# Two relational graph-attention layers: layer 1's keys as columns of the dense products, its softmax by halves of a group, and stage 3's sums in one run

## Chip, core and metric

The kernel runs on one core of a Trainium2 chip. The engines named below are TensorE (PE; its weight loads are PEld), VectorE (DVE), ScalarE (ACT), GpSimd (POOL) and SyncE (SP); SP, ACT and POOL also issue DMAs. The metric is the device time of one execution in microseconds (us), lower is better.

## The reference

`x` is 3125 nodes by 768 features; 53,125 edges (25,000 in both directions and a loop at each node) are sorted by destination and have one of three types. Two layers follow each other, the first with four heads of 192 features and an ELU behind it, the second with one head of 768; then a residual and a layer norm.

```python
xr = einsum('nd,rdf->rnf', x, W)          # three dense products per node
oi, oj = xr[etype, dst], xr[etype, src]   # rows of both ends
alpha = leaky_relu(oi @ q + oj @ k, 0.2)  # a score per edge and head
m = segment_max(alpha, dst)
e = exp(alpha - m[dst])
a = e / (segment_sum(e, dst)[dst] + EPS)
out = segment_sum(a[:, :, None] * oj.reshape(-1, heads, out_ch), dst) + b
```

## The kernel before

Nodes go in 25 blocks of 128. Edges go in 25 groups: group `b` holds up to 17 slots of 128 edges (14 in group 0), and the nodes whose edges it holds. In a slot, the 128 edges lie on the 128 partitions. float32 is multiplied in two parts (`H` and `L`): each product of a block is three matmuls for each of the six 128-feature tiles, so 18 in all.

Four stages follow each other. All instructions are issued in an order written out by hand: each stage has a table `ev` that `when(k, f, ...)` fills, and a loop over `k` that runs what stands under `k` in the order of entry. Each engine takes its own instructions in this order, and waits where the next one's inputs or buffers are not ready.

*Weights and keys.* `weights_kq` loads the 18 tiles of `W1`, splits them into `wH` and `wL`, and multiplies them by `k` and `q`, so that `wk` holds, per relation and head, the vector that gives a node's key or query from `x`. `nodes_kq` then runs over all 25 blocks of `x`: it turns the block (PE transposes), multiplies it by `wk` (L301), puts the keys into the DRAM table `kt1`, and keeps the queries in `qq`. Between these, `first` computes block 0's dense products, 18 pieces of six matmuls, seven of them while `weights_kq` still runs.

*Stage 1* (`phase1`). `d_products` (L750) multiplies blocks 1 to 24 by the 2304 columns of `wH`/`wL`, in pieces of 512 and one of 256 columns over two PSUM banks; `d_row` copies a piece into a row buffer and writes finished rows to the DRAM table `tab1`. A row of `tab1` has, for each of four heads, 192 features and a 1.0, so that a weighted sum of rows also gives the sum of the weights. Beside it run, for groups 0 to 20: the gather of keys, one indirect DMA of 16 bytes an edge per slot (`a_gather`), issued by POOL; the queries (`a_q`, `a_q2`, `a_q3`); the scores, three transposes, two running maxima, exponential and transpose back (`a_alpha`, `a_max`, `a_scan`, `a_back`). The results are the weights `pall`. `w_load` and `w_split` prepare `W2` here.

*Stage 2* (`phase2`). At step `k` POOL gathers slot `k` from `tab1` (L489) into a ring of 14 row buffers. Five steps later `sums` (L1047) adds the slot's rows into the group's nodes: a matmul of 32 columns for each place (a slot and one of the four windows of 32 nodes that it may touch) and head, the four heads side by side in the PE. Its weights `selp` come from `high` (L481), four or eight DVE instructions a slot, three steps ahead. Behind a group's last slot: `e_y` (divides, adds the bias, L1060), `e_x` and `e_h` (ELU), `h_row` (L1126, four writes of the result into layer 2's table `tab2`), `e_t` (turn, L1077), `e_s` and `e_s2` (the two parts `hT`, L1084 to L1099), and layer 2's products for two relations and its keys and queries (L1154), whose 18 steps `d_part` stand between the slots of the next group; `d_row` copies them and writes the rows (L1188) and a tail (L1177), and `d_q` splits the queries into three parts (L156 to L161). All seven writes of a group go into `tab2` at a position read from a register. The last four groups' keys are gathered in stage 2 (`LATE`, `KEYS`, `KEY_AT`), and their softmax runs there (`l_load` to `l_put`), with buffers borrowed from `y`, `ey` and `pt`.

*Stage 3* (`phase3`). Gathers from `tab2` into a ring of 31 rows. The key is column 769 of a row, so scores come from gathered rows (`a_alpha`, L1372). `a_spread` (L1338) and `a_spread2` (L1344) make the selection for the queries in five parts; `a_q2` (L1358), `a_turn` (L1381), `a_scan` (L1387 to L1392), `a_exp` (L1396), `a_back` (L1400), `marks` (L1406), `weigh` (L1420). `sums` (L1433) adds rows in two halves `c` of 384 columns over two PSUM tiles `acc`; `r_own` (ACT, L1444) and `r_other` (DVE, L1450, z in L1455) part the result into R and A, `r_turn` (L1483), `r_high` (L1494) and `r_low` (L1499) turn A, and `d_products` (L1517) multiplies it by the third relation of `W2`. Then residual, layer norm, output. With `e` the step behind a group's last slot, the order is:

```python
for d, f in ((2, a_alpha), (3, a_turn), (4, a_scan), (5, a_exp), (6, a_back), (7, weigh)):
    when(e + d, f, b)
for c in range(2):
    for n in range(8):
        when(e + 9 + 3 * c + n // 3, sums, b, c, n)
    for d, f in ((13, r_own), (13, r_other), (14, r_turn), (15, r_high), (15, r_low)):
        when(e + d + 3 * c, f, b, c)
```

## Time and profile before

| | us |
|---|---|
| median of 2 runs | 2199.07 |
| lowest and highest | 2196.68, 2201.46 |
| the profiled execution | 2202.57 |
| its span, first to last instruction | 2200.7 |
| mean granted PE clock of the span | 0.932 |

The profile is of one execution. Times in it are counted from the first instruction. A line such as "L1060" is a line of the kernel before; a tile is named without its buffer number. In a group, "x100: 406/409/419" is the count and the shortest, middle and longest duration in ns, followed by the first and the last start. A piece of the timeline or of the chain of waits has its start, its length, and in brackets the idle time of the engine before it and what ended that. float32 matmuls of the sums pass through PE twice and have two records each.

### The profile page before, as it was taken

What the parts mean: (1) busy time and instruction counts of PE and PEld (TensorE: products, weight loads), DVE (VectorE), ACT (ScalarE), POOL (GpSimd) and SP (SyncE); (2) the same over time, 40 slices, a digit from 0 to 9 for tenths busy, and PEclk for the clock granted to TensorE, in tenths of its full rate; (3) what the DMA queues carried; (4) which work ended last, traced back from release to release, by engine and by line L of the source; (5) the groups of instructions that cost most, each with busy time, mean ns of one, the idle gap of its engine ahead of it and who ended that gap; (6) DMA issues with size and microseconds to landing.
All of it is one profiled execution on the core that took longest, in us unless ns stands there. A gap on an engine that the chain in (4) does not pass through costs nothing.

```text
span 2200.7 us, 42790 instructions
## 1 busy us (share of the span) xinstructions
PE 1919.3 (87%) x14921; PEld 1328.3 (60%) x14921; DVE 1356.9 (62%) x4864; ACT 443.5 (20%) x978; POOL 1347.3 (61%) x1326
## 2 busy tenths in 40 slices
PE   8999999999979998897979989918888888888886
PEld 7877888778756655554546555704555555555554
DVE  7557566566568765775657657425655656566663
ACT  6412222222101111111111101101222222222222
POOL 4277777777657777665656545054655656666660
PEclk9999999999989999898989989958999999999998
DMA  7476556555878888786868877396878878788880
GB/s 234 146 198 194 182 181 193 173 180 178 268 252 270 280 285 275 223 258 197 261 221 266 253 220 250 126 286 198 267 262 261 270 263 270 262 266 263 273 274 24
DMA packets 173959, 506.28 MB, mean 230 GB/s; under 512 B 52687, under 2 KB 73794, under 8 KB 173733
## 3 DMA queue, kind: packets, MB, share of 16 engines
q0 software_dynamic: 81936, 331.52, 48.4%
q1 hardware_dynamic: 83135, 160.64, 21.4%
q10 hardware_dynamic: 8662, 11.29, 1.6%
q8 instruction: 119, 1.95, 0.4%
q14 instruction: 107, 0.88, 0.1%
HBM read 412.45 MB, written 95.69 MB: 231 GB/s over the span
## 4 chain that ended last, share of the span: by engine, by line
PE 51%; DMA 28%; DVE 13%; ACT 4%; issue 2%; SPq 1%; POOL 1%; POOLq 0%; ACTq 0%; DVEq 0%
PE po L750 16%; DMA ftab<-y 15%; PE acc L1433 12%; PE D L1517 10%; DMA ftab<-r 4%; DVE selp L481 4%; PE po L1154 3%; PE acc L1047 2%; DMA y<-ed_d 2%; DMA kt<-kt,ridx 1%; PE bc L1338 1%; PE bank L301 1%; ACT R L1444 1%; DVE y L1060 1%; DMA d<-dr_d 1%
## 5 line engine op out<-in xcount | busy, mean ns | idle before, releaser
L489 POOL DMA_INDIRECT kt<-kt,ridx x374 | 401.7, 1074 | 121.7 <-issue 71.6
L489 POOL DMA_INDIRECT G<-ftab,ridx x314 | 317.9, 1012 | 201.2 <-PE acc L1433 131.3
L489 POOL DMA_INDIRECT share<-ftab,ridx x299 | 303.3, 1014 | 207.5 <-PE acc L1047 126.6
L750 PE MATMUL po<-wH,xT 128*128 128x512 f32 (+1 forms) x1320 | 391.2, 377 | 0.4 <-DVE xT L729 0.4
L481 DVE TENSOR_SCALAR selp<-frow,fdl,pall 128x32 f32<-128x32 f32 (+1 forms) x1688 | 378.1, 324 | 18.5 <-DMA share<-ftab,rfirst 6.6
L1154 PE MATMUL po<-wH,hT 128*128 128x386 f32 (+1 forms) x1200 | 368.4, 369 | 0.3 <-ACT r L1183 0.3
L1433 PE MATMUL acc<-G,marks 128*32 128x384 f32 (+1 forms) x2520 | 294.7, 493 | 25.5 <-ACT A L1444 25.5
L1154 PEld LDWEIGHTS po<-wH,hT 128*128 128x128 f32 x1200 | 216.7, 193 | 90.7 <-issue 77.9
L750 PEld LDWEIGHTS po<-wH,xT 128*128 128x128 f32 x1320 | 240.2, 190 | 45.9 <-DVE xT L729 1.3
L750 PE MATMUL po<-wL,xT 128*128 128x512 f32 (+1 forms) x660 | 247.0, 374 | 0.0
L1517 PE MATMUL D<-w,AT 128*128 128x512 f32 (+1 forms) x900 | 225.8, 399 | 21.5 <-DVE AT L1499 21.5
L1047 PE MATMUL acc<-share,selp 128*32 128x193 f32 x2936 | 199.5, 351 | 26.5 <-DVE selp L481 26.3
L1154 PE MATMUL po<-wL,hT 128*128 128x386 f32 (+1 forms) x600 | 219.0, 365 | 0.0
L1433 PEld LDWEIGHTS acc<-G,marks 128*32 128x32 f32 x2520 | 142.6, 110 | 126.4 <-ACT A L1444 40.8
L1517 PEld LDWEIGHTS D<-w,AT 128*128 128x128 f32 x900 | 158.3, 216 | 61.1 <-DVE AT L1499 29.0
L489 POOL DMA_INDIRECT g<-ftab,ridx x135 | 137.3, 1017 | 60.9 <-PE acc L1047 39.9
L1344 DVE TENSOR_SCALAR sT<-bc,cols 128x512 bf16<-128x512 f32 (+1 forms) x125 | 82.9, 663 | 121.5 <-PE bc L1338 121.5
L1183 ACT COPY r<-po 128x384 f32<-128x384 f32 (+3 forms) x125 | 49.4, 412 | 537.2 <-PE po L1154 342.0
L1047 PEld LDWEIGHTS acc<-share,selp 128*32 128x32 f32 x2936 | 81.9, 112 | 107.3 <-DVE selp L481 57.6
L1433 PE MATMUL acc<-share,marks 128*32 128x384 f32 (+1 forms) x464 | 136.9, 490 | 3.5 <-ACT A L1444 3.5
L750 PEld LDWEIGHTS po<-wL,xT 128*128 128x128 f32 x660 | 125.0, 189 | 22.3
L1154 PEld LDWEIGHTS po<-wL,hT 128*128 128x128 f32 x600 | 115.6, 193 | 37.0 <-issue 37.0
(303 smaller groups left out, 2455.2 us busy)
## 6 DMA issues: line engine op xcount, KB each, us to landing
ftab<-share SPq DMA_DIRECT2D x71, 386.0 KB
ftab<-r SPq DMA_DIRECT2D x49, 386.0 KB
w_d<-w2hl SPq DMA_DIRECT2D x18, 768.0 KB
sT<-dr_d SPq DMA_DIRECT2D x25, 544.0 KB
share<-in_L_gnn_W_dram SPq DMA_DIRECT2D x30, 384.0 KB
share<-in_x_dram SPq DMA_DIRECT2D x27, 384.0 KB
xb_d<-share SPq DMA_DIRECT2D x25, 384.0 KB
ftab<-y SPq DMA_DIRECT2D x100, 96.0 KB
```

The costliest lines, as they stand in the source:

```text
L301: T.matmul(to, a[:, 2 * i + f, :], t[:, f, :w], start=(n == 0), stop=(n == 2 * DT - 1))
L481: return V.tensor_scalar(sel.rearrange("p (t f) -> p t f", f=32), of, dl[:, b, j:j + 1], p, op0=ALU.is_equal, op1=ALU.mult)
L489: return G.indirect_dma_start(out=to, out_offset=None, in_=tab, in_offset=_index(i[:, j:j + 1]), bounds_check=NP * R - 1, oob_is_err=False)
L750: m = T.matmul(po[:, :n], xT[:, s, t, :], w[:, t, KQ + f:KQ + f + n], start=(i == 0), stop=(i == 3 * DT - 1))
L1047: i_ = T.matmul(acc[32 * h:32 * h + 32, t // 2, t % 2 * CW:(t % 2 + 1) * CW], sel[:, h, 32 * n:32 * n + 32], g[:, h * CW:(h + 1) * CW], st ...
L1060: V.scalar_tensor_tensor(y[:, w, :F1], acc[:, w // 2, w % 2, :F1], rz[:, w // 2, w % 2:w % 2 + 1], bias1, op0=ALU.mult, op1=ALU.add)
L1154: T.matmul(po[:, :n], hT[:, k, t, :], w[:, t, f:f + n], start=(i == 0), stop=(i == 3 * DT - 1))
L1183: S.copy(o[:, at:at + m], po[:, got:got + m])
L1338: T.matmul(bc[:, :n], one, s["d"][:, 4 * i * P:4 * i * P + n], start=True, stop=True)
L1344: V.tensor_scalar(s["sT"][:, 4 * i * P:4 * i * P + n], bc[:, :n], cols[:, b:b + 1], None, op0=ALU.is_equal)
L1433: m = T.matmul(s["acc"][u][32 * t:32 * t + 32, c, :HALF + c], s["marks"][:, at_.index((j, w)), :], row_at(base(b) + j)[:, c * HALF:][:, :H ...
L1517: T.matmul(s["D"][:, f:f + n], s["AT"][:, k, t * P:(t + 1) * P], w2[:, t, w, f:f + n], start=(i == 0), stop=(i == 3 * DT - 1))
```

## The change

Layer 1's keys and queries are columns of its dense products. The weights are kept as `weights[0]` and `weights[1]`; a relation's 768 columns become 772, with a key column behind each head where the row of `tab1` had its 1.0, and 12 query columns stand at the end. `nodes_kq`, `kt1` and the key gathers go. Products are six pieces of 386 columns (the last 398), for all 25 blocks; `d_row` copies a piece as it is and writes it as half a row. The first six pieces, of blocks 0 and 1, run inside `weights_kq`. In stage 1 the queries go to `pall`, and no scores are computed.

In stage 2 the ring has 23 rows. A group goes by halves, slots 0 to 7 and 8 to 16 (`CUT`): `alpha` adds the gathered key columns to the queries and then sets them to 1.0; `turn`, `scan`, `back`; `marks` and `weigh` make the weights in few wide DVE instructions; `sums` adds all places of the half in one run. Layer 2's products are four pieces.

In stage 3 both halves' sums of a group are issued as one run; the loads of the third relation's weights go to ACT's queue; the two local arrays `one` and `d` have 128 partitions, of which all but the first are zero; the key is column 768 and the 1.0 column 769.

```diff
+    EARLY = 6
+    GB = NB - 4
+    NX, NG = 14, 26
...
+    WA, WB = 2 * RW, RW + H1 * R
+    PIECES1 = [(0, i * HW, HW) for i in range(4)] + [(1, 0, HW), (1, HW, WB - HW)]
+    PIECES2 = [(i * HW, min(HW, 2 * (D + R) - i * HW)) for i in range(4)]
...
+    def d_row(o, q, b, p, po):
+        S.copy(o[:, :HW], po[:, :HW])
+        to = tab1[b * P * R:(b + 1) * P * R, :].rearrange("(p r) f -> p r f", r=R)
+        nc.sync.dma_start(to[:, p // 2, p % 2 * HW:(p % 2 + 1) * HW], o[:, :HW])
+        if p == len(PIECES1) - 1:
+            q1s = q.tile([P, H1 * R, 3], BF, name="q1s", bufs=2)
+            split3([q1s[:, :, i] for i in range(3)], po[:, HW:HW + H1 * R], q, [P, H1 * R])
+            nc.sync.dma_start(q1_d[b * P:(b + 1) * P, :], q1s.rearrange("p k s -> p (k s)"))
...
+        def alpha(b, u):
...
+            i, e = (0, CUT + 1) if u == 0 else (CUT + 1, slots(b))
+            for i_, e_, g in stretches(ring, lambda j: base(b) + j, i, e):
+                key = g.rearrange("p n (h f) -> p n h f", h=H1)[:, :, :, F1]
+                V.tensor_add(a[:, i_:e_], pall[:, b, i_:e_], key)
+                V.memset(key, 1.0)
+            V.scalar_tensor_tensor(als[b % 2][:, 1 + i:1 + e], a[:, i:e], NEG_SLOPE, a[:, i:e], op0=ALU.mult, op1=ALU.max)
...
+        def weigh(b, u):
...
+                V.tensor_tensor(sel[:, i:e], st["marks", b][:, off + i:off + e, None, :].to_broadcast([P, e - i, H1, 32]),
+                                p[:, j - a:j - a + e - i, :, None].to_broadcast([P, e - i, H1, 32]), op=ALU.mult)
...
         def d_row(b, p):
...
+            S.copy(o[:, c * HW:c * HW + n], po[:, :n])
+            if p == 1:
+                s["q"] = work.tile([P, R], F32, name="q2", bufs=2)
                 t = tails[b % 2]
+                V.tensor_copy(t[:, 0:1], po[:, n:n + 1])
+                V.tensor_copy(s["q"][:, 0:2], po[:, n + 1:n + 3])
                 nc.sync.dma_start(s["rows"][:, WHOLE, D:], t)
+            if p == 3:
+                V.tensor_copy(s["q"][:, 2:3], po[:, n:n + 1])
+                split3([q2s[:, b, :, i] for i in range(3)], s["q"], work, [P, R])
+            if c == 1:
+                nc.sync.dma_start(s["rows"][:, r, :], o)
...
+        for b in range(NB):
+            when(base(b) + 9 if b else 3, marks, b)
+            for u, k in ((0, base(b) + 13), (1, base(b) + slots(b) + 4)):
+                when(max(k - 12, 0), f_load, b, u)
+                for d, f in ((0, alpha), (0, turn), (1, scan), (2, back), (3, weigh), (3, sums)):
+                    when(k + d, f, b, u)
+            for d, f in ((7, e_y), (7, e_x), (9, e_h), (9, h_row), (11, e_t), (11, e_s), (11, e_s2)):
+                when(k + d, f, b)
+            for m in range(18):
+                n = k + 13 + m * 7 // 11 if m < 11 else k + 21 + (m - 11) * 4 // 7
+                when(n, d_part, b, m)
+                for p in range(4):
+                    if 4 * m < 18 * (p + 1) <= 4 * m + 4:
+                        when(n + 1, d_row, b, p)
...
-            nc.sync.dma_start(w2[p:p + 64, t].bitcast(F32), w2_d[i:i + 64, :].rearrange("p (s f) -> p s f", s=2))
+            nc.scalar.dma_start(w2[p:p + 64, t].bitcast(F32), w2_d[i:i + 64, :].rearrange("p (s f) -> p s f", s=2))
...
+        def sums(b):
...
+            for c in range(2):
+                for u in range(2):
+                    o = rounds(b, u)
+                    for j, w in o:
...
+            if b < 2:
+                q = [(2 + 12 * b + 2 * i, 3 + 12 * b + 2 * i) for i in range(5)]
+                q += [(12 + 12 * b, 13 + 12 * b, 14 + 12 * b)]
+            else:
+                q = [(base(b) + i - (i == 0), base(b) + i) for i in range(5)]
+                q += [(base(b) + 4, base(b) + 6, base(b) + 8)]
...
+            for d, f in ((4, a_alpha), (4, a_turn), (5, a_scan), (5, a_exp), (6, a_back), (6, weigh), (7, sums)):
                 when(e + d, f, b)
+            for d, f in ((10, r_own), (12, r_other)):
+                when(e + d, f, b, 0)
+            for d, f, *c in ((14, r_own, 1), (16, r_turn, 0), (16, r_high, 0), (16, r_other, 1), (16, r_low, 0),
+                             (16, r_turn, 1), (16, r_high, 1), (16, r_z), (16, r_low, 1), (17, r_z2), (18, r_plus)):
+                when(e + d, f, b, *c)
+            for i in range(6):
+                when(e + 17 + i, d_part, b, i)
+            for d, f in ((24, e_y), (25, e_n), (26, e_sd), (27, e_low), (27, e_out)):
                 when(e + d, f, b)
```

In stage 3 a group is 17 steps, so that `d_part` of one group (17 to 22) stands on steps 0 to 5 of the next, ahead of that group's `a_turn` (4), `a_back` (6) and `sums` (7).

More of the change, by code (lines that the diff above doesn't have):

```diff
@@ L986, in l_alpha @@
[L986 to L1001 removed]
+        landed = {}
@@ L1035, in sums, with back @@
[L1035 to L1045 removed]
+        def back(b, u):
+            e = st.pop(("e", b, u))
+            n = e.shape[0]
+            T.transpose(st["pa", b, u][:, 3 * P:3 * P + n], e, ident[:n, :n])
@@ L1046, in sums @@
                 for h in range(H1):
-                    i_ = T.matmul(acc[32 * h:32 * h + 32, t // 2, t % 2 * CW:(t % 2 + 1) * CW],
-                                  sel[:, h, 32 * n:32 * n + 32], g[:, h * CW:(h + 1) * CW], start=((j, t) == first),
+                    i_ = T.matmul(acc[c][32 * h:32 * h + 32, t % 2 * CW:(t % 2 + 1) * CW], sel[:, mine.index((j, t)), h, :],
+                                  row_at(base(b) + j)[:, h * CW:(h + 1) * CW], start=((j, t) == own[0]),
                                   stop=((j, t) == last), skip_group_check=True)
-                    tc.declare_no_dep(i_.ins, rows_of, reason="the selection waits for the rows")
+                    tc.declare_no_dep(i_.ins, landed[b, j], reason="the ones of this slot wait for its rows")
@@ L1220, in phase2 @@
                 gather(k)
[L1221 to L1228 removed]
             for f, a in ev.get(k, []):
                 f(*a)
[L1231 removed]
+            if k == NK + 12:
                 for b in range(len(xbs)):
```

860 lines of the change are left out of this document (298 added, 562 removed).

## The prediction

> **What bounds the kernel now.** I read the stages first (busy time by stretch, cut where the groups of one line end and the next begin), then the periods inside the two gathering stages, then the chain of waits.
>
> ```profile
> span 2200.7 us, 42790 instructions
> ...
> 0.00:51.50 51.50, 44.19 (x318) 40.59 (x319) 41.01 (x96) 34.55 (x63) 25.79 (x28) 1.00 0.75 241
> 51.50:105.30 53.80, 51.58 (x391) 48.03 (x390) 28.82 (x85) 26.20 (x64) 11.41 (x31) 1.00 0.51 151
> 105.30:620.00 514.70, 497.31 (x2792) 410.66 (x2792) 315.59 (x1020) 111.35 (x348) 384.46 (x354) 0.99 0.62 193
> 620.00:1432.40 812.40, 713.96 (x6641) 457.30 (x6638) 541.06 (x2280) 98.93 (x232) 496.02 (x490) 0.93 0.76 243
> 1432.40:1488.50 56.10, 6.87 (x33) 2.03 (x33) 19.00 (x97) 0.31 (x1) 32.86 (x31) 0.50 0.99 295
> 1488.50:2200.70 712.20, 605.38 (x4754) 369.65 (x4753) 411.46 (x1288) 172.20 (x271) 396.79 (x392) 0.92 0.73 242
> ```
>
> Columns: length, busy us of PE, PEld, DVE, ACT, POOL, then granted clock, DMA share, GB/s. The rows are: weights; the pass over the nodes for keys and queries; layer 1's products; stage 2 (gather, sums, layer 2's products); a gap; stage 3. Products are bound by PE (497 of 515 us). The gap is bound by DMA, with PE idle at half clock.
>
> ```profile
> L1060 DVE SCALAR_TENSOR_TENSOR y<-acc,rz,fbias x100: 406/409/419, 647.0 to 1407.1; 128x192 f32<-128x192 f32 x100
> L489 POOL DMA_INDIRECT share<-ftab,rfirst x38: 994/998/1020, 623.0 to 1486.4; - x38
> ...
> 708.53 2.98 DMA ftab<-y
> ...
> 753.37 4.80 DMA ftab<-r
> ...
> 797.03 4.20 DMA ftab<-y
> ...
> 1689.19 7.44 PE acc L1433 x80
> ...
> 1717.10 7.44 PE acc L1433 x80
> ```
>
> Four of these L1060 belong to a group, so 25 groups begin between 647.0 and about 1405.9: 24 periods of 31.6 us. In quiet stretches (chain, 708.53 to 797.03, three periods) a period is 29.5 us, and the chain there is the seven writes into layer 2's table, one behind the other: four of the elu rows at 3 to 4.2 us, two result rows at about 4.8 us, one small tail. The surplus of 2 us a period is the softmax of the last four groups, which is squeezed in between. Stage 3 goes at 27.9 us a group (1689.19 to 1717.10) along PE.
>
> **Stages 0 and 1.** The pass over the nodes goes (53.8 us). Of block 0's 108 products in it and before it, 42 stood in the weights' stretch; now all 108 products of the first six pieces stand there, with two blocks' turns.
>
> ```profile
> 896.14 0.51 PE L1154 MATMUL po<-wH,hT 128*128 128x386 f32 x2
> 896.49 0.33 PE L1154 MATMUL po<-wL,hT 128*128 128x386 f32 x1
> ```
>
> ```profile
> 314.97 0.82 PE L721 MATMUL px<-fident,xr 128*128 128x128 f32 x6
> ```
>
> Two 386-wide products take 0.35 us here, so 0.176 us each: 66 more are 11.6 us, two blocks' turns at most 1.6 us, and the stretch ends at 64.7 us. A block of stage 1 took 514.7/24 = 21.4 us for 18 times 2304 columns; it becomes 18 times 2328, 1% more, and loses its softmax turns and PE's wait for their exponentials. 108 x 0.176 = 19.0 us is the floor, 21.6 the ceiling; I take 20.6, near the old pace, since turns and query products stay. 64.7 + 24 x 20.6 = 559 us against 620: **-61 us** (-70 to -37). The half rows are two writes where one was; SP is idle enough, and the removed key gathers free POOL, which bounds nothing here.
>
> **Stage 2.** Keys now arrive with the rows, so score, softmax and weighting of each half stand between the gathers and its sums, in all 25 groups. Engines go in the order written. I follow one period.
>
> ```profile
> 734.81 0.55 DVE L1115 TENSOR_SCALAR ey<-ey 128x768 f32<-128x768 f32 x1
> 735.86 0.96 DVE L1118 SCALAR_TENSOR_TENSOR y<-y,ey 128x768 f32<-128x768 f32 x1
> 741.55 0.59 ACT L1084 CAST hT<-pt 128x512 fp32r<-128x512 f32 x1
> 743.41 0.85 DVE L1099 TENSOR_TENSOR hT<-pt,hT 64x256 fp32r<-64x256 f32 x2
> 750.76 0.38 DVE L156 CAST q2s<-q 128x3 bf16<-128x3 f32 x1
> 751.77 0.17 DVE L161 CAST q2s<-c 128x3 bf16<-128x3 f32 x1
> 898.12 0.86 PE L1047 MATMUL acc<-g,selp 128*32 128x193 f32 x16
> 898.91 0.44 PE L1154 MATMUL po<-wH,hT 128*128 128x386 f32 x1
> 1684.08 0.49 PE L1381 MATMUL pa<-fident,al 128*17 128x128 f32 x3
> 1686.61 0.31 ACT L1396 ACTIVATE e<-e 17x128 f32<-17x128 f32 x1 [7.99 <-DVE e L1392]
> 1687.64 0.23 PE L1400 MATMUL pa<-fident,e 17*128 17x17 f32 x1
> 1687.91 1.35 DVE L1420 TENSOR_TENSOR marks<-marks,pa 128x544 f32<-128x544 f32 x4 [0.85 <-PE pa L1400]
> 1708.54 0.18 DVE L1372 TENSOR_TENSOR a<-qe,G 128x17 f32<-128x17 f32 x1
> ```
>
> Prices: turn, scans and exponential 2.84 us (1684.08 to 1686.92), the same length of line in stage 2; back 0.23. Weighting: 30 places x 32 values took 1.35 us, 1.4 ns a value; a half now has 13 or 10 places x 128 values, 2.0 or 1.5 us with fewer starts. Sums: 16 records are two places in 0.79 us, of which the switch of shape is about 0.1; 0.33 a place, so 4.4 and 3.4 us. Splitting the queries 1.18, with its copy 1.35; the elu steps 734.81 to 736.82, 2.0; hT's high and low parts 741.55 to 744.26, 2.7, of which 2.15 lie behind the exponential that ACT has first. Scores: about four instructions of 0.18, 0.7.
>
> In the written order a period runs: 32 products of the previous group (5.6), turn to exponential of half 1 (2.84, with 12 products beside it), back, weighting (2.0), sums (4.4), the last 28 products (4.9). Then DVE's queue holds the split of those products' queries, the elu steps of this group, and only behind them the scores of the next group's half 0: 1.35 + 2.0 + 0.7, in which PE has nothing, because its next instruction is that half's turn, and the group's own turn, sums and products stand behind it. Then turn to exponential 2.84, hT's parts 2.15, weighting 1.5, sums 3.4. Sum: 5.6 + 2.84 + 0.23 + 2.0 + 4.4 + 4.9 + 4.05 + 2.84 + 2.15 + 1.5 + 3.4 = 33.9, and some 0.6 in hand-overs: 34.5 us. Gathers do not set it: the deeper ring lets them run half a period ahead. Nor do the writes, whose 29.5 us now lie beside it.
>
> PE then waits some 2.2, 4.0 and 3.5 us in a period. What that costs in clock, stage 3 shows:
>
> ```profile
> 1697.75 0.51 PE L1433 MATMUL acc<-G,marks 128*32 128x385 f32 x1 [1.16 <-ACT A L1444]
> ...
> 1704.94 0.61 PE L1462 MATMUL bc<-z,both 128*128 128x1 f32 x4 [1.81 <-DVE sT L1344]
> 1705.41 0.52 PE L1483 MATMUL D<-fident,A 128*128 128x128 f32 x3
> ...
> 1707.09 2.22 PE L1517 MATMUL D<-w,AT 128*128 128x512 f32 x6 [0.84 <-DVE AT L1499]
> ...
> 1707.96:1711.37 3.41, 3.41 (x9) 1.94 (x8) 1.69 (x4) 0.00 (x0) 2.80 (x3) 0.50 0.91 286
> ```
>
> After waits of only 1.2, 1.8 and 0.8 us the clock is at 0.50 for 3.41 us, a loss of 1.7. The Trainium skill ("TensorE: Matmul & The Clock Gate", Part 1) says the clock halves after an idle window of about 3.4 us and that gaps under about 3 us are safe; this trace disagrees, no single gap here being that long, so the measurement decides. For stage 2 I take one such window, 1.7 us, as in stage 3 (bounds none and two): **36.2 us** a period.
>
> Head: the first L1060 stood 24.0 us behind the first gather (623.0 to 647.0); half 1's chain adds 0.7 + 2.84 + 0.23 + 1.5 + 3.4, less the last slot's sums it had anyway: 32. Tail as before, 1405.9 to 1432.4, 26.5. 32 + 24 x 36.2 + 26.5 = 927 against 809.4: **+118 us** (-43 at the writes' pace, +161 with two windows).
>
> **The gap.**
>
> ```profile
> 1450.59 22.78 DMA d<-dr_d
> ...
> 1458.57 1.00 POOL L489 DMA_INDIRECT G<-ftab,rfirst  x1 [2.09 <-DMA G<-ftab,rfirst]
> ```
>
> The loads of the third relation's weights leave SP's queue for ACT's, which is idle until the first exponential, so the local rows no longer land at 1473.4. Next late is the fourteenth gather, issued at 1458.57 beside the same loads; with some 5 us to land (a row write of its size takes 4.8) and about 5 for scores to weights, the sums start near 1469 in place of 1488.5, a half-clock start costs 1.7, and the second half of each group follows the first sooner: **-22 us** (0 to -30).
>
> **Stage 3.** The sums now stand before any reading of them.
>
> ```profile
> 1703.49 0.61 DVE L1450 SCALAR_TENSOR_TENSOR A<-acc,half,A 128x384 f32<-128x384 f32 x1
> ...
> 1706.48 0.56 DVE L1499 TENSOR_TENSOR AT<-D,AT 128x384 fp32r<-128x384 f32 x1 [0.54 <-ACT AT L1494]
> ```
>
> The 1.16 us wait goes: there the second half of the sums waited for ACT reading other columns of the same PSUM tile, so waits go by whole tile. But by the same rule everything behind the sums comes late together: four of L1450 at 0.57 to 0.61, z 0.2, the first low part 0.56, only then the second turn, and from it to the products 1.68 (1705.41 to 1707.09): 4.8 us, in which PE has 1.4 of turns and small products, so 3.4 idle. Ahead of the sums, the products now stand before the turn and not beside the softmax: turn to exponential 2.84, with another 0.6 of marks and selection ahead of the scans, back 0.23, weighting 1.35, less 0.7 + 0.6 of work: 3.6 idle. 7.0 against 1.16 + 1.81 + 0.84 = 3.8: 31.1 us a group, I take 31.0. **+74 us** (0 if the tile rule doesn't hold for the turned block and the softmax is covered, +115 with a second half-clock window).
>
> **Sum.** The profiled execution took 2202.6 us, 1.9 around its span; the median of the runs is 2199.1. 2202.6 - 61 + 118 - 22 + 74 = 2311.6; 3.5 less for the median: **2308 us**, +5%.
>
> **Rivals.** (A) Faster: DVE's waits are covered, and stage 2 runs at the pace of its seven writes in a row, 29.5 us, without the late groups' surplus. For it speaks that they fill the quiet periods now; against it that the split and the elu steps stand ahead of the scores in DVE's order. It decides if scores come before PE has finished the last products. 2202.6 - 61 - 22 - 43 + 0 - 3.5 = 2073 us. (B) No change: no half-clock window in stage 2 (-41) and stage 3 as before (-74): 2193 us. The clock gate's rule named above, taken at its word, leads here if the gaps stay below its window; the trace's own half-clock rows speak against it. (C) A second half-clock window in each period of both gathering stages: +43 + 41, 2392 us.
>
> **Numbers.** Forecast 70%, A 13%, B 12%, C 5%. About 2% (44 us) is what this kernel's measurement tells from no change. The forecast's own range is 2250 to 2350, all slower; with 1 in 100 of it falling short, slower is 0.74, same 0.13, faster 0.13. The range that leaves out A and C, 18%, is 2175 to 2365.
>
> **What would show it.** Layer 1's products ending near 559; the first gather behind them; the elu writes spaced 36 us and no longer back to back; PE idle behind DVE's scores of half 0 for about 4 us a period; half clock in each; stage 3's first sums at about 36 us behind the last row written, and 31 us between groups. Wrong if elu writes still follow each other without a gap, or if PE's waits in stage 2 stay below 2 us.

## The result: slower by 8%, and the profile after

The changed kernel takes 2375.48 us (median of 2 runs, 2374.77 to 2376.19) against 2199.07: 1.080 times as long, 95% interval 1.075 to 1.0855. The forecast was 2308 us, 2175 to 2365: the direction held, the time lies 10 us above the upper end.

The profile after, by stretch: length, busy us of PE, PEld, DVE, ACT, POOL, then granted clock, DMA share, GB/s. The rows are the weights, the first blocks' rest, layer 1's products, the head of stage 2 (first gather to first elu reading, L839), its 24 periods, its tail, the gap, stage 3, and the last group's end.

```profile
0.00:65.10 65.10, 51.61 (x332) 47.42 (x332) 37.59 (x98) 33.61 (x63) 21.69 (x20) 0.95 0.43 137
65.10:105.00 39.90, 38.41 (x220) 37.07 (x219) 12.66 (x39) 6.83 (x14) 5.67 (x10) 1.00 0.65 214
105.00:567.60 462.60, 458.81 (x2914) 454.03 (x2912) 267.80 (x987) 95.26 (x175) 0.00 (x0) 0.99 0.58 190
567.60:615.20 47.60, 14.88 (x236) 9.62 (x236) 22.82 (x71) 1.05 (x3) 28.19 (x27) 0.61 0.78 268
615.20:1511.00 895.80, 637.69 (x6502) 531.52 (x6503) 377.63 (x1150) 101.47 (x238) 396.76 (x395) 0.82 0.65 208
1511.00:1540.50 29.50, 22.73 (x108) 21.20 (x106) 7.06 (x25) 4.84 (x10) 0.00 (x0) 0.83 0.32 101
1540.50:1591.50 51.00, 6.29 (x32) 2.11 (x33) 19.74 (x96) 0.31 (x1) 24.77 (x24) 0.52 0.97 268
1591.50:2341.40 749.90, 595.82 (x4711) 414.20 (x4711) 400.56 (x1229) 170.29 (x268) 404.59 (x398) 0.89 0.70 233
2341.40:2373.00 31.60, 9.02 (x43) 7.51 (x43) 6.19 (x17) 1.57 (x4) 1.04 (x1) 0.66 0.04 13
```

Stage 1 is still PE at work (459 of 463 us). In the 24 periods of stage 2 PE is busy 71% of the time where it was 89% (672 of 758.9 us), and its clock fell from 0.93 to 0.82. Put beside the forecast's terms (the first gather stands at 570.9, 623.0 before; the last group's first L839 at 1511.2):

| stretch, us | before | after | forecast of the change | measured |
|---|---|---|---|---|
| until the first gather | 623.0 | 570.9 | -61 | -52.1 |
| head of stage 2 | 24.0 | 44.3 | +8 | +20.3 |
| 24 periods of stage 2 | 758.9 | 896.0 | +110 | +137.1 |
| tail of stage 2 | 26.5 | 29.3 | 0 | +2.8 |
| gap | 56.1 | 51.0 | -22 | -5.1 |
| stage 3 | 712.2 | 781.5 | +74 | +69.3 |
| sum | 2200.7 | 2373.0 | +109 | +172.3 |

So 63 us are missing: 27 in the periods (37.33 us and not 36.2), 17 in the gap, 12 in the head, 9 ahead of it, 3 in the tail, and stage 3 came out 5 better. No single term makes the miss.

**One period of stage 2.** The timeline of the changed kernel: start, length, engine, in brackets the idle time before and what ended it.

```profile
905.58 3.57 PE L825 MATMUL acc<-share,sel 128*32 128x193 f32 x80 [1.63 <-DVE sel L806]
...
908.94 1.19 PE L825 MATMUL acc<-g,sel 128*32 128x193 f32 x24
...
915.85 0.16 DVE L946 COPY q<-po 128x1 f32<-128x1 f32 x1 [3.86 <-ACT r L938]
...
917.97 0.96 DVE L885 SCALAR_TENSOR_TENSOR y<-y,ey 128x768 f32<-128x768 f32 x1
918.85 0.21 DVE L747 TENSOR_TENSOR a<-pall,g 128x36 f32<-128x36 f32 x1
...
919.44 0.80 PE L756 MATMUL pa<-fident,al 128*32 128x128 f32 x3 [4.19 <-DVE al L749]
...
922.70 0.31 PE L775 MATMUL pa<-fident,e 32*128 32x32 f32 x1 [0.75 <-ACT e L770]
...
926.55 5.88 PE L825 MATMUL acc<-g,sel 128*32 128x193 f32 x80 [3.54 <-DVE sel L806]
```

This is the order that the forecast followed: behind the products DVE takes the queries' last part (from 915.85) and the elu (to 918.9), and only then half 0's scores (918.85). PE waits 4.19 us there, and 3.54 behind the turn back while ACT and DVE make hT's parts and the weights. What differs is the price of the sums: half 1's 104 records take 4.5 us, half 0's 80 take 5.9. The next rows (length, PE busy, granted clock) say why:

```profile
914.44:917.85 3.41, 0.81 (x5) 1.00 0.99 259
917.85:921.26 3.41, 1.82 (x9) 0.50 0.89 326
921.26:924.68 3.42, 1.00 (x5) 0.50 0.44 148
924.68:928.09 3.41, 1.54 (x20) 0.50 0.18 42
928.09:931.50 3.41, 3.41 (x48) 0.50 0.79 187
931.50:934.91 3.41, 3.41 (x38) 1.00 0.87 309
...
951.99:955.40 3.41, 0.64 (x4) 1.00 0.91 264
955.40:958.82 3.42, 1.53 (x8) 0.50 0.91 340
```

Not one window of 3.41 us is at half clock but four in a row, 13.65 us, because PE fills none of the first three; the clock comes back only behind the fourth, which it fills. Half 0's sums fall into it.

**The head.** Same view, around the first scores:

```profile
588.54 0.67 PE L569 MATMUL pq<-q,sT 128*128 128x36 bf16 x17 [4.90 <-DMA q<-q_d]
...
590.14 0.79 DVE L584 TENSOR_REDUCE pall<-tq 128x68 f32<-128x612 f32 x1
...
592.77 0.21 DVE L747 TENSOR_TENSOR a<-pall,share 128x36 f32<-128x36 f32 x1
```

The last four groups' queries, whose rows come out of the last products, are made one after the other until 590.9, and DVE has them ahead of the first scores. In the kernel before, the same four steps came at 561.5, 581.8, 611.2 and 623.3 (its first gather stands at 623.0), and the first group's sums waited for none of them.

**The gap.**

```profile
1570.57 1.00 POOL L374 DMA_INDIRECT G<-ftab,rfirst  x1 [2.46 <-DMA G<-ftab,rfirst]
...
1586.73 0.18 DVE L1108 TENSOR_TENSOR a<-qe,G 128x14 f32<-128x14 f32 x1 [20.72 <-DMA G<-ftab,rfirst]
...
1591.48 4.91 PE L1170 MATMUL acc<-G,marks 128*32 128x384 f32 x38
```

The fourteenth gather (1570.57, counted from 1542.46) is issued 30 us behind the last row (forecast 26) and its rows are used 16 us later, where I had put 5; from scores to sums 4.7 (I had 5). DMA is at 0.97 all the while: the third relation's weights, 12 loads of 384 KB, run beside the gathers on whichever queue they stand.

**Stage 3.** The timeline of one period:

```profile
1701.31 0.55 PE L1220 MATMUL D<-fident,A 128*128 128x128 f32 x3 [1.62 <-DVE AT L1236]
...
1703.08 0.59 PE L1074 MATMUL bc<-d,one 128*128 128x512 bf16 x1 [0.88 <-DVE rz L1205]
...
1715.47 0.23 PE L1136 MATMUL pa<-fident,e 17*128 17x17 f32 x1 [2.13 <-ACT e L1132]
...
1729.84 0.55 PE L1220 MATMUL D<-fident,A 128*128 128x128 f32 x3 [0.78 <-DVE A L1187]
```

And the windows of 3.41 us in it, columns as above:

```profile
1699.51:1702.92 3.41, 1.06 (x9) 1.00 0.83 246
1702.92:1706.33 3.41, 3.25 (x8) 0.50 0.91 325
...
1713.16:1716.57 3.41, 0.98 (x21) 1.00 0.88 305
1716.57:1719.98 3.41, 3.41 (x22) 0.50 0.73 248
```

PE waits 1.62, 0.88, 2.13 and 0.78 us (6.2 in all with two small ones; I had 7.0), and two windows of each period are at half clock, not one, each behind a window with about 1 us of work.

### The profile page after: what moved, and what is told of

The parts are those of the page before. It is cut to its first block, busy times and chain, and to the rows that moved or that the text cites. A ratio compares the mean times of both kernels' runs of the same rounds, so it can differ in the third digit from the quotient of the medians.

```text
span 2373.0 us, 40808 instructions
## 1 busy us (share of the span) xinstructions
PE 1835.2 (77%) x15090; PEld 1524.7 (64%) x15091; DVE 1152.0 (49%) x3707; ACT 415.2 (17%) x774; POOL 882.7 (37%) x875
## 5 line engine op out<-in xcount | busy, mean ns | idle before, releaser
L374 POOL DMA_INDIRECT G<-ftab,ridx x314 | 319.0, 1016 | 246.1 <-PE acc L1170 172.3
L919 PE MATMUL po<-waH,hT 128*128 128x386 f32 (+1 forms) x1200 | 321.9, 346 | 1.0 <-ACT hT L863 0.7
L464 PE MATMUL po<-waH,xT 128*128 128x386 f32 x1104 | 301.5, 346 | 7.6 <-ACT share L472 7.4
L919 PEld LDWEIGHTS po<-waH,hT 128*128 128x128 f32 x1200 | 217.7, 190 | 16.9 <-issue 14.7
L825 PE MATMUL acc<-g,sel 128*32 128x193 f32 x2736 | 158.8, 395 | 77.5 <-DVE sel L806 77.5
L464 PEld LDWEIGHTS po<-waH,xT 128*128 128x128 f32 x1104 | 205.7, 191 | 8.7 <-ACT share L472 8.7
L919 PE MATMUL po<-waL,hT 128*128 128x386 f32 (+1 forms) x600 | 204.1, 340 | 0.0
L464 PE MATMUL po<-waL,xT 128*128 128x386 f32 x552 | 189.0, 342 | 0.0
L825 PEld LDWEIGHTS acc<-g,sel 128*32 128x32 f32 x2736 | 107.8, 132 | 117.6 <-DVE sel L806 81.3
L464 PE MATMUL po<-wbH,xT 128*128 128x386 f32 (+1 forms) x552 | 147.9, 342 | 0.0
L825 PE MATMUL acc<-share,sel 128*32 128x193 f32 x1840 | 105.5, 389 | 48.9 <-DVE sel L806 48.9
```

What stands on the lines that cost most here:

```text
L374: return G.indirect_dma_start(out=to, out_offset=None, in_=tab, in_offset=_index(i[:, j:j + 1]), bounds_check=NP * R - 1, oob_is_err=False)
L464: T.matmul(po[:, :n], xt[b][:, s, t, :], weights[k][w][:, t, f:f + n], start=(i == 0), stop=(i == 3 * DT - 1))
L825: i_ = T.matmul(acc[c][32 * h:32 * h + 32, t % 2 * CW:(t % 2 + 1) * CW], sel[:, mine.index((j, t)), h, :], row_at(base(b) + j)[:, h * CW:( ...
L919: T.matmul(po[:, :n], hT[:, k, t, :], weights[0][w][:, t, f:f + n], start=(i == 0), stop=(i == 3 * DT - 1))
```

## The experiments

Theories: (1) in stage 2, DVE's order makes PE's waits around half 0, and the half clock that they bring costs more than the one window I had priced; (2) in stage 3, likewise, a second window; (3) head and gap as read above. Against them: half 0 waits for its gathered rows; the half clock lies beside waits and costs little; the longer stage 3 comes from the new layout and not from the order.

The fifteen runs were made on four occasions. On two of them the kernel before took 2193 and 2195 us, as at first, on the other two 2441: there every kernel is slower, and only stretches of runs of one occasion are compared.

**First occasion (before: 2440.65 us).** Fillers in stage 2: `busy(n)` is n matmuls of the unit matrix into the first PSUM bank of the products, which is free at both places.

```diff
+            when(k + 25, busy, 15)
...
+                if u == 0:
+                    when(k + 2, busy, 13)
```

> Stage 2's two long waits of PE are filled: 15 matmuls of 128 columns stand ahead of half 0's turn, 13 behind its turn back, into a PSUM bank that is free there; nothing else is moved. Theory, that the four windows of 3.41 us at half clock in each period (13.65 us from 917.85 in the changed kernel) are what the forecast's single window missed: they go, half 0's 80 records of sums take about 3.5 us and not 5.9, its three turns 0.5 and not 0.8, the period falls from 37.3 to about 34.4 us, and the time by 24 x 2.9 = 70 to about 2305 us. Rival, that the clock costs the one window that I had priced, 1.7 us: period 35.6, time 2334. Second rival, that half clock lies beside waits and costs nothing: 2375.

Half 0 early:

```diff
-            for u, k in ((0, base(b) + 13), (1, base(b) + slots(b) + 4)):
+            for u, k in ((0, base(b) + 8), (1, base(b) + slots(b) + 4)):
```

> Half 0's scores, turn, running maxima, weights and sums stand five steps earlier, so that they come ahead of the previous group's elu steps and of the split of the queries in DVE's order, and PE has the last 28 products of the group before beside them. Theory, that the order on DVE makes the wait of 4.2 us ahead of the turn and the 3.5 us behind it: both go, the half-clock stretch with them, and the period falls from 37.3 to between 27 and 31 us, where the seven writes in a row (29.5 us before) may set it: 2175 to 2225 us. Rival, that half 0 waits for its gathered rows: period about 37, time about 2375.

Fillers in stage 3, into PSUM tiles that are done with:

```diff
+            if b:
+                when(e + 5, fill, b - 1, 8, "acc")
...
-            for d, f, *c in ((14, r_own, 1), (16, r_turn, 0), (16, r_high, 0), (16, r_other, 1), (16, r_low, 0),
-                             (16, r_turn, 1), (16, r_high, 1), (16, r_z), (16, r_low, 1), (17, r_z2), (18, r_plus)):
+            for d, f, *c in ((14, r_own, 1), (15, fill, 3, "pa"), (16, r_turn, 0), (16, fill, 6, "pa"), (16, r_high, 0), (16, r_other, 1), (16, r_low, 0),
+                             (16, r_turn, 1), (16, r_high, 1), (16, r_z), (16, fill, 3, "pa"), (16, r_low, 1), (17, r_z2), (18, r_plus)):
```

> Stage 3's waits are filled with matmuls of 128 columns: 3 ahead of the first turn of A, 6 behind it, 3 behind the sums of z, 8 ahead of the turn back of the weights; nothing is moved. Theory, that the second half-clock window in each period of stage 3 (two of 3.41 us, one from 1702.92 and one from 1716.57) is dear: without both the period falls from 30.7 to about 27.5 us and the time by 24 x 3.2 = 77 to about 2298. Rival, that the waits themselves make the longer period and the clock lies beside them: 30 us or more, 2350 to 2375.

Stage 3 in the old order, the one quoted for the kernel before, with the sums again in its rounds and readings behind each half:

```diff
-            for d, f in ((4, a_alpha), (4, a_turn), (5, a_scan), (5, a_exp), (6, a_back), (6, weigh), (7, sums)):
+            for d, f in ((2, a_alpha), (3, a_turn), (4, a_scan), (5, a_exp), (6, a_back), (7, weigh)):
                 when(e + d, f, b)
...
+            for c in range(2):
+                for n in range(8):
+                    when(e + 9 + 3 * c + n // 3, sums, b, c, n)
```

> Stage 3 is issued in the order of the kernel before (the sums in two halves of columns with the readings behind each, the scores earlier, the products from step 19), with the rest of the changed kernel. Theory, that the order alone makes stage 3 longer: a group takes 27.3 to 27.9 us again and not 30.7, and the time falls by some 70 to about 2305 us. Rival, that the selection over 128 partitions, the wider sums or the ring of rows make it: 30 us or more, 2360 to 2375.

Measured: 2706.9, 2600.0, 2760.9 and 2640.1 us. Since each kernel alters one stage, the others give the unaltered pace on this occasion: stage 2 43.6 us a period (runs that altered stage 3), stage 3 37.0 (runs that altered stage 2). Against these: fillers in stage 2 44.4, half 0 early 39.6; fillers in stage 3 39.7, old order 34.6. The timeline of the run with fillers in stage 3 shows what is different here, in a stage 2 that is the changed kernel's:

```profile
1014.66 3.11 PE L825 MATMUL acc<-g,sel 128*32 128x193 f32 x40 [1.64 <-DVE sel L806]
...
1021.23 0.54 PE L825 MATMUL acc<-share,sel 128*32 128x193 f32 x5 [0.18 <-issue]
...
1023.38 0.34 PE L919 MATMUL po<-waH,hT 128*128 128x386 f32 x1 [0.52 <-issue]
```

Half 1's sums, from 1014.66 to the products behind them at 1023.38, take 8.7 us in place of 4.5. One half-clock window (1015.26 to 1018.67) falls into them, which accounts for at most 1.7; for the rest the profile names nothing that PE waits for. That its own instructions come late is the likely reason, but only argued. The orders showed their sign (half 0 early gains 4.0 us a period, the old order 2.4), the fillers, which add some 1,400 matmul records to stage 2 and 1,000 to stage 3, could not.

**Second occasion (before: 2192.99 us).** The changed kernel again, both fillers, half 0 early, and five edits together.

> The changed kernel as it is, for comparison on the chip of these runs: the chip of the four runs ahead of this one took 2441 us for the kernel before, where the first took 2199, and in its records PE waits for its own instructions. If this chip is like the first: 2375 us, period of stage 2 37.3 us, of stage 3 30.7. If it is like the second: about 2750 us, 44 and 37 us, the pace of the untouched stages in the four runs.

2374.2 us, 37.33 and 30.7 us a period: like the first time.

> The fillers of the two earlier runs together: 15 and 13 matmuls of 128 columns in stage 2's two long waits, 3, 6, 3 and 8 in stage 3's. Theory, that the stretches at half clock are on the path and no others: stage 2's period 34.4 against 37.3 us, stage 3's 27.5 against 30.7, together 24 x 6.1 = 146 us less, 2230. Rival, that the clock costs no more than one window of 1.7 us a period in each stage: 2290. Second rival, as on the second chip, that PE runs short of instructions and the fillers only add to them: not faster than the changed kernel on the same chip.

2284.0 us, which as a time is the rival's (2290) and not the theory's (2230). Stage 2's period is 36.36 and stage 3's 27.9. The rows are those of two lines in this kernel (count, shortest, middle, longest ns, first and last start). Four L839 belong to a group, 1.0 us from first to last, so (1493.1 - 1.0 - 619.4)/24 = 36.36. In stage 3 a group has two readings into A, 1.1 us apart, so (2252.6 - 1.1 - 1582.8)/24 = 27.9.

```profile
L839 DVE SCALAR_TENSOR_TENSOR y<-acc,rz,fbias x100: 405/407/418, 619.4 to 1493.1; 128x192 f32<-128x192 f32 x100
...
L1190 DVE SCALAR_TENSOR_TENSOR A<-acc,half,A x50: 606/609/618, 1582.8 to 2252.6; 128x384 f32<-128x384 f32 x50
```

Stage 3 as one stretch, columns as in the first fence:

```profile
1585.00:2250.00 665.00, 622.07 (x5525) 474.24 (x5526) 393.13 (x1198) 166.74 (x261) 390.62 (x387) 1.00 0.76 256
```

The same reading in the changed kernel, (2340.9 - 1.1 - 1604.1)/24 = 30.65 us:

```profile
L1187 DVE SCALAR_TENSOR_TENSOR A<-acc,half,A x50: 606/609/619, 1604.1 to 2340.9; 128x384 f32<-128x384 f32 x50
```

In stage 3 the clock is at 1.00 throughout, and 2.8 us a period are gone: theory (2) holds. In stage 2 only 1.0 us went, less than the rival's 1.7, but by turns: periods of 34.7 us, into which no window at half clock fell, and of 36.8 and 38.5, into which one or two stretches did. Two of PE's waits were left open there, so for stage 2 the run settles nothing.

> Half 0's scores five steps earlier, once more, beside the changed kernel on the same chip. Theory, that DVE's order makes PE's two waits around half 0: stage 2's period falls by at least 6 us from 37.3, to 31 or less, and the time by 150 or more, to 2225. On the second chip it fell from 44 to 40. Rival, that only part of the waits goes since a group's sums wait for the elu's reading of the last ones: 33 to 35 us, 2265 to 2320.

2180.2 us, 0.9942 of the kernel before (0.9925 to 0.9959). The period is 29.15 us, 8.2 less: theory (1)'s first part holds, and half 0 did not wait for rows. Timeline: the scores' chain now stands beside the last products, PE waits 1.09 us ahead of half 0's sums and not 8.5, and these take 3.5 us.

```profile
911.37 0.49 PE L756 MATMUL pa<-fident,al 128*32 128x128 f32 x3
...
915.56 1.54 DVE L806 TENSOR_TENSOR sel<-marks,pa 128x1024 f32<-128x1024 f32 x2
...
916.82 3.48 PE L825 MATMUL acc<-share,sel 128*32 128x193 f32 x80 [1.09 <-DVE sel L806]
```

The five edits (stage 3 in the old order is left out of the diff):

```diff
-            for u, k in ((0, base(b) + 13), (1, base(b) + slots(b) + 4)):
+            for u, k in ((0, base(b) + 8), (1, base(b) + slots(b) + 4)):
...
+                h = 3 if u == 1 else 0
-                for d, f in ((0, alpha), (0, turn), (1, scan), (2, back), (3, weigh), (3, sums)):
+                for d, f in ((-h, alpha), (-h, turn), (1 - h, scan), (0 if h else 2, back), (1 if h else 3, weigh), (3, sums)):
...
-                                      + [(b, p) for p in range(6) for b in last], due)
+                                      + [(b, p) for p in (5, 0, 1, 2, 3, 4) for b in last], due)
...
-            q = max(c + 1, 6 * b + 2) if b < GB else max(6 * NB - 5, c + 2) + 2 * (b - GB)
+            q = max(c + 1, 6 * b + 2) if b < GB else max(6 * NB - 22, c + 2) + 2 * (b - GB)
...
+                if f == 0:
+                    tc.add_manual_dep(m.ins, landed[0, SLF - 1], whole_dep, reason="the first group's rows come first")
...
+        when(SLF, w_rest)
```

> Five edits, each in a stretch of its own: half 0's scores five steps earlier, half 1's scores and turn three; stage 3 in the order of before; the query piece of the last four blocks' products first and their queries formed beside the other pieces; the third relation's weights loaded behind the first group's gathers. By theory: the head of stage 2 falls from 44 to some 36 us, its period from 37.3 to 28 to 31 (the seven writes in a row), the gap from 51 to some 35, stage 3 by 70: 2375 - 8 - 24 x 7.5 - 16 - 70 = about 2100 us, less than both kernels. Rivals: the gathers of group 1 are late instead (gap and the first period of stage 3 together as before, 2116); the period stays above 34 (2190).

2139.2 us. In this kernel the second layer's weights are loaded over the first's while the last four blocks' products still read them, so those blocks' rows are other ones; the products wait for these loads and end at 623 us and not at 567. Stage 2's period is 28.4 us, stage 3's 27.3. From stage 3's first gather to its first sums it takes 52 us, 49 in the changed kernel: ACT, which issues the loads, was held by them for 24 us (1404.68 to 1428.94), and the exponential of the first group stands behind them.

**Third occasion (before: 2441.02 us).** Four filled waits; head and gap alone; the five edits with the second layer's loads four steps later and the third relation's on SP; the same with stage 3's waits filled.

```diff
+            when(k + 25, busy, 17)
...
+                if u == 0:
+                    when(k + 2, busy, 6)
                 for d, f in ((0, alpha), (0, turn), (1, scan), (2, back), (3, weigh), (3, sums)):
                     when(k + d, f, b, u)
+                when(k + 2, busy, *((14,) if u == 0 else (5, 1)))
```

> In stage 2 alone, all four waits of PE are filled: 17 matmuls of 128 columns ahead of half 0's turn, 6 between the turn of the elu rows and half 0's turn back, 14 behind that, 5 behind half 1's turn back. With two waits filled (the run with both fillers) the period went 34.7, 36.8 and 38.5 us by turns: 34.7 where no window at half clock fell into it, 1.8 more for each stretch that did. Theory, that without half clock the period is 34.7 us, the 34.5 of my sum, and that the clock's share of the changed kernel's 37.3 to 37.5 is 2.7 us where I had put 1.7: every period 34.7 to 35.2, the time 2374 - 24 x 2.5 = 2314 us. Rival, that other waits grow as these go: above 36 in every period, 2345 or more.

> The changed kernel with its head of stage 2 and its gap altered: the query piece of the last four blocks' products first and their queries formed beside the other pieces (the second layer's weights are loaded four steps later for it); the third relation's weights loaded by SP behind the first group's last gather. Theory, that the last four groups' queries, whose steps stand on DVE until 590.9 us, held the head, and the weights' bytes beside the gathers held the gap: first elu reading some 36 us behind the first gather in place of 44.4, first sums of stage 3 some 28 to 32 us behind the first gather in place of 48 to 49, in all 25 us less, 2350. Rivals: the head waits for the rows of half 0 in any case (43 or more); what the gap gains stage 3's first periods lose (time as before).

```diff
-                when(TAIL + 4 * p + 5, second_weights, r, f, n)
+                when(TAIL + 4 * p + 9, second_weights, r, f, n)
...
-                m = nc.scalar.dma_start(w2[p:p + 64, t].bitcast(F32), w2_d[i:i + 64, :].rearrange("p (s f) -> p s f", s=2))
+                m = nc.sync.dma_start(w2[p:p + 64, t].bitcast(F32), w2_d[i:i + 64, :].rearrange("p (s f) -> p s f", s=2))
```

> The five edits together, with the second layer's weights loaded four steps later, behind the pieces that still use the first's, and the third relation's loads on SP: products end near 568 us and not at 623, the head some 36 us, stage 2's period 28.4, the gap some 30, stage 3's period 27.4. 2139 - 55 - 4 - 20 = about 2060 us, 6% under the kernel before. Rival, that the loads' new place makes stage 3's first periods longer: 2080.

```diff
+            for d, n in ((11, 4), (16, 6), (18, 3)):
+                when(e + d, fill, b, n)
```

> As the run with all edits mended, and stage 3's waits filled with 4, 6 and 3 matmuls of 128 columns (between the sums of the two halves, ahead of the sums of z, ahead of the products). Theory, that with one window at half clock gone stage 3's period falls from 27.3, eight windows of 3.41, by the 1.7 us that it costs to 25.6: 41 us less, about 2020. Rival, that the matmuls delay what they stand ahead of, or the period is held by the gathers (17 at 1.3 us are 22, and the DMA share is 0.79): 27 or more, 2060.

2688.2, 2686.8, 2513.2 and 2585.4 us; as on the first occasion the times say little. Of the stretches, those that hang on DMA and DVE are plain: with head and gap altered, first gather to first L839 took 56.0 us where the run with filled waits, unaltered there, took 63.6, and stage 3's first gather to its first sums 29.5 against 48.3. So theory (3) holds for what made these two stretches long. But its rival for the gap holds too: "what the gap gains stage 3's first periods lose". The first period of stage 3 takes 53.6 us where it took 36.9, so that the second group's sums start 87.4 us behind the first gather and not 88.7, and the time is the same (2686.8 and 2688.2 us). In that period PE waits for local rows of a later group, whose load stands behind the weights' in SP's order:

```profile
1777.51 0.61 PE L1080 MATMUL bc<-d,one 128*128 128x512 bf16 x1 [18.51 <-DMA d<-dr_d]
```

**Fourth occasion (before: 2195.17 us).** Three of the last four once more.

> The four filled waits of stage 2 once more: in the last four runs every kernel, the one before too (2441 us), ran as on the first occasion where PE waits for its instructions, and more matmuls say nothing there. Where the kernel before takes some 2199 us: theory, that the clock's share of the changed kernel's period of 37.3 us is 2.6 and the rest is the 34.5 of my sum: every period 34.7 to 35.2 us, the time 2311 to 2320. Rival, that half clock is worth the 1.7 that I had put or less, and other waits grow: 35.6 us or more a period, 2334 or more.

2313.0 us, as theory (1) had it. The row of L839 gives (1455.4 - 1.0 - 617.6)/24 = 34.87 us a period:

```profile
L839 DVE SCALAR_TENSOR_TENSOR y<-acc,rz,fbias x100: 406/409/420, 617.6 to 1455.4; 128x192 f32<-128x192 f32 x100
```

The clock of stage 2 stands at 1.00:

```profile
640.00:1450.00 810.00, 762.57 (x8234) 685.85 (x8236) 368.87 (x1126) 98.83 (x232) 380.85 (x379) 1.00 0.68 221
```

And in the timeline half 0's sums take 3.5 us again:

```profile
911.06 3.47 PE L825 MATMUL acc<-g,sel 128*32 128x193 f32 x80 [0.29 <-DVE sel L806]
```

So without half clock a period is 34.9 us, and half clock costs 37.33 - 34.87 = 2.5, net of what the fillers themselves may add.

> The five edits together once more, where the kernel before takes some 2199 us. On the slow occasion the gap fell from 49 to 36 us and the head from 63 to 58. Theory: head some 38 us, stage 2's period 28.4 us, gap 30 to 36, stage 3's period 27.4: about 2065 us, 0.94 of the kernel before. Rival, that stage 3's first periods give back what the gap gains: 2080.

2093.2 us, 0.9543 of the kernel before (0.9516 to 0.957): less than both kernels, on this occasion; on the third it was 1.030 of the kernel before (1.026 to 1.034). Head 38 us (573.0 to 611.1), period 28.7, first gather to first sums in stage 3 30.5, stage 3's period 27.3. But the 18 us by which the first sums of stage 3 come sooner are all given back in its first period, 54.9 us long (from the first reading of one group's sums to that of the next). Between the sums of the first group PE waits for local rows again:

```profile
1399.43 0.61 PE L1081 MATMUL bc<-d,one 128*128 128x512 bf16 x1 [25.77 <-DMA d<-dr_d]
```

The second group's sums start 87.3 us behind the first gather, in the first run with five edits 83.6, in half 0 early, which loads the weights beside the first gathers, 80.5. So the rival written down for this run (2080 us) holds against its theory (2065): no run shows a gain in time from moving the weights' loads behind the first gathers.

> The five edits and stage 3's three filled waits once more, where the kernel before takes some 2199 us. Theory, that stage 3's period falls from 27.3 us, eight windows of 3.41 with one at half clock, by the 1.7 us that this window costs: 25.6, 41 us less than the run with the five edits. Rival, that another chain holds the period, or the matmuls stand in its way: 27 us or more, no gain.

2087.6 us, 0.9518 (0.9491 to 0.9545): not to be told from the run before it. The period went from 27.3 to 27.1 us, not to 25.6, though the clock stands at 1.00 from 1440 to 2050: in the old order the window at half clock costs 0.2 us net of the fillers. Its rival stands; what then holds the 27 us was not tried.

## Why the forecast was right, and where it was wrong

**Stages 0 and 1** (-61, measured -52): right in kind, the products are bound by PE. A block takes (567.1 - 65.1)/24 = 20.9 us and not 20.6, which makes most of the 9 missing us. The first gather stands 3.8 us behind the start of the last product; in the kernel before it was 3.3 (619.6 to 623.0).

**Stage 2, the chain** (34.5 us without clock): right, 34.9 measured with the clock full, and not by luck: PE's two long waits are 4.19 and 3.54 us (forecast 4.0 and 3.5), the sums 4.5 and, at full clock, 3.5 (4.4 and 3.4). That DVE's split and elu ahead of the scores make PE's longest wait is shown by half 0 early, which takes 8.2 us off.

**Stage 2, the clock: the term of the sum that was mis-sized most.** "For stage 2 I take one such window, 1.7 us" cost 2.5 (four windows, not one): 0.76 x 24 = 18 of the 63 missing us, and the chain's 0.37 x 24 = 9 beside it. I carried the single window over from stage 3, though my own waits of 4.0 and 3.5 us stand close behind each other there, with only turns between them: PE could fill no window in that stretch, and the half clock lasted until it filled one. The Trainium skill ("TensorE: Matmul & The Clock Gate", Terms) prices throttled time at the share of the clock that it loses, which would be 6.8 us for 13.65 at half clock; the runs disagree, 2.5 measured. By the rows above PE is busy for 7.8 of the 13.65 us and waits for the rest in any case. What grew is the work that the next step waits for: half 0's sums, 5.9 us for 3.5.

**Head** (32, measured 44): the sum had the new chain but not the queries of the last groups, which lose their cover when the products' queries come last. That is 7.5 us in the run with head and gap alone. In the five edits the first scores stand 15.4 us behind the first gather (572.98 to 588.38) and wait for gathered rows, in the changed kernel 21.8 (570.93 to 592.77); how much of the rest of the head is due to half 1's earlier scores there was not tried.

**Gap** (-22, measured -5): the step that failed is "some 5 us to land": 16, at a DMA share of 0.97. The loads' bytes beside the gathers make that: moved behind them, they let the first sums start 18 us sooner. The queue matters as well, for what stands behind the loads on it: ACT's exponential waited there for 24 us, and with the loads back on SP the local rows made PE wait for 25.8, as 22.78 us of such a load stood in the chain of the kernel before. The changed kernel, whose loads stand on ACT ahead of any exponential, has neither (3.7 us for local rows at most), as forecast.

**Stage 3** (+74, measured +69): the size is right in part by luck, its split wrong. The 27.9 us were read from a quiet stretch; over all groups the kernel before takes (2172.6 - 1499.3)/24 = 28.05. A group became 2.6 us longer (30.65), which makes 62 us; the other 7 lie ahead of the first group's first reading and behind the last one's, where I had put none. I gave 3.1 us a group to waits and left the clock at one window. But with the clock full the new order takes 27.87 us and the old one, in the same layout, 27.13, both with fillers. So the waits add some 0.7, and the two windows cost 2.8. That the order makes it and not the new layout is shown by the five edits: the old order in the changed kernel's layout takes 27.3.

**The rivals.** A (the writes' pace) needed scores ahead of the products' end: half 0 early is that case, and comes to 29.15 us. But the five edits reach 28.7, so the 29.5 us of the seven writes are not the floor that I took them for. B fell in both stages. C, a second half-clock window in each period, 2392 us with a chance of 5%, was nearest: in stage 3 it is word for word what happened, in stage 2 it is four windows that cost one and a half. That its time is near is partly luck: it comes to 38.0 and 32.7 us a period, where 37.3 and 30.65 were measured, and head, gap and products made up for that. The range ended at 2365 because it left C out, while head, gap, clock and products all came out dearer than their terms. Three slips in the working decide nothing: a floor of 19.0 us a block makes the first range begin at -99 and not -70, C's 43 us for stage 2 are 24 x 1.7 = 41, and the 3.6 us idle ahead of stage 3's sums add up to 3.7.

## What to carry to other kernels

Where a step moves between a load and its use, read who is ahead of it in each engine's order, not only how long it takes: one number in the order list (13 to 8) was worth 194 us here. Price half clock by the work that falls between two windows that PE fills, not by the count of gaps. A load that is not needed yet costs its bytes beside the gathers, whatever queue it stands on, and it holds what stands behind it on that queue; after moving it, look at the second group and not only at the first.

## What the runs showed of the hardware

The clock goes by windows of 3.41 us on a fixed grid. In the changed kernel's records 80 windows at full clock were followed by half clock, and PE was busy at most 0.44 of each; none that stayed at full clock was below 0.50. At half clock a window of 0.81 still did not bring full clock back, one of 0.90 did; in other runs the two overlap (0.88 did not in the run with both fillers, 0.82 did in the five edits). (In the kernel before, a few windows of up to 0.64 were followed by half clock, so the busy share of the records isn't all of it.) The Trainium skill ("TensorE: Matmul & The Clock Gate", Part 1) has the same free-running window, and there the trace agrees; but it asks for an idle one, and "Why this matters for your kernels" on the same page calls gaps under about 3 us safe; here 0.98 of 3.41 us busy was idle enough, with no gap in it over 2.13.

Loops with half clock in every turn can settle on whole windows. In the changed kernel stage 2's stretches begin at 917.85 and 955.40, 37.55 us or eleven windows apart, and all 23 from 640 to 1500 are spaced so; stage 3's periods are nine windows (30.7) and in the old order eight (27.3). With the clock full they are no such multiple (34.9). It need not be one number: in stage 3 of the kernel before the half-clock stretches come eight and nine windows apart by turns (28.05 us in the mean), and in stage 2 of half 0 early there are mostly 17 windows to two periods (28.2 and 29.9 us). So in such a loop a gain may show only in whole windows; no run tested that.

On two occasions of four, every kernel that ran on both kinds took 11 to 24% longer. In the profiled variants all of it lies behind layer 1's products (which ended near 567 us there too), and for a part of PE's lost time the profile names no cause. The order of the kernels was another as well: half 0 early and the five edits, which are ahead of the kernel before on an ordinary occasion, were 1.065 and 1.030 of it there. What sets these occasions apart was not found. The record has the same chip number, 12, for the first occasion and the second, so the chip, which the expectations name, is not shown to be it.
